# Attention on one core: half a slot of logits placed ahead of the value products, and the end of a query tile taken off ScalarE

## The chip, the cores and the metric

The kernel runs on one core of a Trainium2 chip. The metric is the device time of one execution in microseconds (us), as the median of several runs. The core has five engines with a queue each: TensorE (PE, matrix products; its weight loads are shown apart as PEld), VectorE (DVE), ScalarE (ACT), GpSimd (POOL) and SyncE (SP, which issues the DMAs here). Each engine works through its own queue in order, and semaphores tie the queues together.

## What is computed

The input x has the shape (2, 256, 64, 64): 2 images of 256 channels and 4096 tokens. Layer 0 is a Mamba block with an MLP; the change does not touch it. Layer 1 is attention with 8 heads of 32 channels, and this is what the change is about:

```python
x = x + _L0_conv_ref(_gn(x), ...)
x = x + _L1_conv_ref(_gn(x), qkv_w, qkv_b, 8)
...
qkv = jnp.einsum('bchw,oc->bohw', x, qkv_w) + qkv_b[None, :, None, None]
attn_logits = jnp.einsum('bhci,bhcj->bhij', q, k) * scale
attn_weights = jax.nn.softmax(attn_logits, axis=-1)
out = jnp.einsum('bhij,bhcj->bhci', attn_weights, v)
```

The kernel takes exponentials of the scaled logits without subtracting a maximum, sums them, and divides the value products by the sums at the end of a tile. A check of the range at the very end (`out_of_range`) starts a slower version if a sum was too large.

## The kernel before

`mamba_stage` runs first and fills about 2100 us. Then `attention_block` runs once for each image. Inside it, `prepare` normalises x and projects it to q, k and v; q and k go through DRAM, v stays in SBUF. What follows is one long loop of slots, and the change is in this loop.

**Tiles and slots.** A block has KG = 2 groups of four heads and NT = 8 query tiles of T = 512 queries, so 16 query tiles. Each tile goes through NC = 32 chunks of 128 keys. One slot s is one chunk of one tile: i is the tile, c the chunk. There are S = 512 slots in a block and 1024 in all.

**The work of one slot.**
- `logits(s)` (L952): on TensorE four products of keys and queries (L963), one for each head of the group, each 128 keys by 512 queries. Two heads share one PSUM tile `s`; the pool `ps_s` has two such tiles (L830), one for heads 0-1 and one for heads 2-3 in turn.
- `exponentials(s)` (L972): on ScalarE two activations (L977), each over two heads (128 x 1024), from a tile `s` into a tile `e`. The pool `ep` has six tiles `e` (L845), so those of three slots.
- `values(s)` (L980): on TensorE the products of v with `e` (L986), one for each head, added up over the 32 chunks in one PSUM tile `po` (one buffer, `ps_o`). The profile shows each of them as two matmuls, so eight for a slot.
- `add_up(s)` (L995): the sums of exponentials. DVE adds the `e` of heads 0-1 to `acc` (L1007). POOL adds the `e` of heads 2-3 to `acc_p` (L1018); in the 13 slots of `SHARED`, POOL takes one head of it (L1016) and DVE the other (L1015).

**The end of a tile.** `finish(i)` (L1020) is a generator; `side.run()` (L1074) advances it by one `yield` a slot, or two slots later where it yields 2. Its steps: copy `acc` (DVE, L1026), add the shared parts (DVE, L1027, which reads POOL's `acc_p`), copy `po` (ScalarE, L1029), and start the load of `res`, the old x (SP, L1031). Then sum over the partitions by products with ones (TensorE, L1036), copy the sums (DVE, L1039), and add the bias to `res` (ScalarE, L1040). Then reciprocals in four parts (DVE, L1047), `po` times the reciprocal (POOL, L1050), `res` plus `po` (POOL, L1052), and the store (SP, L1053).

**What sets the order.** Within `tc.manual_schedule()` the instructions of each engine stand in the order of the Python code, and the framework adds the semaphores. The loop (L1058 to L1078) issues for a slot s: on ScalarE both exponentials of s; on TensorE the values of s - 1, then a step of `finish` if one is due, then both halves of the logits of s + 1; then `add_up(s)`. When i is the last tile of the first group (i = 7), the keys of the next group are loaded as well, one piece every four slots (L1066). The SP queue carries these loads, the loads of queries (at c = 0, for the next tile) and those of `res`.

Of the kernel before, what the change touches and what calls it, by code (L numbers as in the profile page):

```python
# [13 lines left out]
AF = mybir.ActivationFunctionType  # L14
ALU = mybir.AluOpType
# [4 lines left out]
P = 128  # L20
# [793 lines left out]
def attention_block(ctx, tc, b, stats, consts, w, out, scratch, range_t):  # L814
# [5 lines left out]
    nc = tc.nc  # L820
    ident, gmat, _, eps_t = consts
    C, L = out.shape
    KC = C // P
    NT = L // T
    NC = L // P
    SCALE = 1.0 / math.sqrt(D)
# [10 lines left out]
    b_qkv = wp.tile([P, 3 * KC], F32, name="b_qkv")  # L837
# [4 lines left out]
    p1 = ctx.enter_context(tc.tile_pool(name=f"l1p1{b}", bufs=1))  # L842
    p2 = ctx.enter_context(tc.tile_pool(name=f"l1p2{b}", bufs=2))
    kp = ctx.enter_context(tc.tile_pool(name=f"l1k{b}", bufs=NT + 1))
    ep = ctx.enter_context(tc.tile_pool(name=f"l1e{b}", bufs=6))  # L845
    keys = {}
    queries = {}

    def load_keys(g, t):
        k = keys[g, t] = kp.tile([P, 4, T], F32R, name="k")  # L850
        load_stack(nc, k, scratch.qk[b * KG + g, 1, t], 1)

    def load_queries(i):
        if i < KG * NT:
            g, t = divmod(i, NT)
            q = queries[i] = p2.tile([P, 4, T], F32R, name="q")
            load_stack(nc, q, scratch.qk[b * KG + g, 0, t], 0)

    def s_tile():
        return ps_s.tile([P, 2, T], F32, name="s", tag="s")  # L860
# [79 lines left out]

    class Slot:
        pass

    S = KG * NT * NC
    SHARED = range(6, NC, 2)
    todo = {}
    tiles = {}
    side = Slots()  # L950

    def logits(s):  # L952
        if s >= S:
            return
        i, c = divmod(s, NC)
        kt, kj = divmod(c * P, T)
        d = todo[s] = Slot()
        d.s = []
        for half in range(2):
            ps = s_tile()  # L960
            for j in range(2):
                h = 2 * half + j
                nc.tensor.matmul(  # L963
                    ps[:, j, :],
                    lhsT=keys[i // NT, kt][:, h, kj : kj + P],
                    rhs=queries[i][:, h, :],
                    start=True,
                    stop=True,
                )
            d.s.append(ps)  # L970

    def exponentials(s):  # L972
        d = todo[s]
        d.e = []
        for half in range(2):
            e = ep.tile([P, 2, T], F32, name="e")
            nc.scalar.activation(e, d.s[half], AF.Exp, scale=SCALE)  # L977
            d.e.append(e)

    def values(s):  # L980
        i, c = divmod(s, NC)
        g = i // NT
        if c == 0:
            tiles[i].po = ps_o.tile([P, T], F32, name="po")
        for h in range(4):
            nc.tensor.matmul(  # L986
                tiles[i].po[h * D : (h + 1) * D, :],
                lhsT=v[:, c, g * P + h * D : g * P + (h + 1) * D],
                rhs=todo[s].e[h // 2][:, h % 2, :],
                start=(c == 0),  # L990
                stop=(c == NC - 1),
            )
        del todo[s]

    def add_up(s):  # L995

        i, c = divmod(s, NC)
        tile_ = tiles[i]
        ea, eb = todo[s].e
        if c == 0:  # L1000
            tile_.acc = ps_a.tile([P, 2, T], F32, name="acc")
            tile_.acc_p = p2.tile([P, 2, T], F32, name="acc_p")
            nc.vector.tensor_copy(tile_.acc, ea)
            tile_.eb0 = eb
            return
        acc, acc_p = tile_.acc, tile_.acc_p
        nc.vector.tensor_add(acc, acc, ea)  # L1007
        if c == 1:
            nc.gpsimd.tensor_add(acc_p, tile_.eb0, eb)  # L1009
        elif c in SHARED:  # L1010
            if c == SHARED[0]:
                tile_.acc_2 = ps_2.tile([P, T], F32, name="acc_2", tag="a2")
                nc.vector.tensor_copy(tile_.acc_2, eb[:, 0, :])
            else:
                nc.vector.tensor_add(tile_.acc_2, tile_.acc_2, eb[:, 0, :])  # L1015
            nc.gpsimd.tensor_add(acc_p[:, 1, :], acc_p[:, 1, :], eb[:, 1, :])  # L1016
        else:
            nc.gpsimd.tensor_add(acc_p, acc_p, eb)  # L1018

    def finish(i):  # L1020

        g, t = divmod(i, NT)
        d = tiles[i]
        cols = bass.ts(t, T)
        acc = p1.tile([P, 3, T], F32, name="acc_sb")
        nc.vector.tensor_copy(acc[:, 0:2, :], d.acc)  # L1026
        nc.vector.tensor_add(acc[:, 2, :], d.acc_2, d.acc_p[:, 0, :])  # L1027
        po = p1.tile([P, T], F32, name="po_sb")
        nc.scalar.copy(po, d.po)  # L1029
        res = p2.tile([P, T], F32, name="res")  # L1030
        nc.sync.dma_start(res, x[g * P : (g + 1) * P, cols])  # L1031
        yield
        ps = ps_2.tile([P, T], F32, name="sums_ps", tag="a2")
        for h in range(4):
            part = acc[:, h, :] if h < 3 else d.acc_p[:, 1, :]
            nc.tensor.matmul(ps[h * D : (h + 1) * D, :], lhsT=ones, rhs=part, start=True, stop=True)  # L1036
        yield
        sums = p1.tile([P, T], F32, name="sums")
        nc.vector.tensor_copy(sums, ps)  # L1039
        nc.scalar.activation(res, res, AF.Identity, bias=b_qkv[:, 2 * KC + g : 2 * KC + g + 1])  # L1040
        yield
        at = b * KG * NT + i
        nc.vector.tensor_reduce(range_t[:, 0, at : at + 1], sums, AX.X, ALU.max)
        yield 2
        r = p1.tile([P, T], F32, name="r")
        for j in range(T // P):
            nc.vector.reciprocal(r[:, bass.ts(j, P)], sums[:, bass.ts(j, P)])  # L1047
            yield 2
        nc.vector.tensor_reduce(range_t[:, 1, at : at + 1], r, AX.X, ALU.max)
        nc.gpsimd.tensor_mul(po, po, r)  # L1050
        yield 2
        nc.gpsimd.tensor_add(res, res, po)  # L1052
        nc.sync.dma_start(out[g * P : (g + 1) * P, cols], res)  # L1053

    with tc.manual_schedule():
        logits(0)
        s = 0
        while s <= S or side.waiting:  # L1058
            i, c = divmod(s, NC)
            if s < S:  # L1060
                if c == 0:
                    tiles[i] = Slot()
                    load_queries(i + 1)
                if i % NT == NT - 1 and i < KG * NT - 1 and c % (T // P) == 0:

                    load_keys(i // NT + 1, c * P // T)  # L1066
                exponentials(s)
            if 1 <= i <= KG:
                nc.sync.dma_start(scratch.v[b * KG + i - 1, :, c, :], v[:, c, (i - 1) * P : i * P])
            if 0 < s <= S:  # L1070
                values(s - 1)
                if c == 0:
                    side.start(side.now, finish(i - 1))
            side.run()  # L1074
            logits(s + 1)
            if s < S:
                add_up(s)
            s += 1  # L1078
# [99 lines left out]
@with_exitstack  # L1178
def conv_preact_kernel(ctx: ExitStack, tc: tile.TileContext, x: bass.AP, w: dict, out: bass.AP):
    nc = tc.nc  # L1180
    B, C, L = x.shape
    KC = C // P
    NT = L // T

    const = ctx.enter_context(tc.tile_pool(name="const", bufs=1))
    ident = const.tile([P, P], F32, name="ident")
    make_identity(nc, ident)
    gmat = const.tile([P, P], F32, name="gmat")
    nc.sync.dma_start(gmat, w["group_mean"])
    lnmat = const.tile([P, P], F32, name="lnmat")  # L1190
    nc.vector.memset(lnmat, 1.0 / C)
    eps_t = const.tile([P, 1], F32, name="eps_t")
    nc.vector.memset(eps_t, EPS)
    consts = (ident, gmat, lnmat, eps_t)

    scratch = Scratch(ctx.enter_context(tc.tile_pool(name="scratch", bufs=1, space=DRAM)), B * KG, L)
    range_t = const.tile([P, 2, B * KG * NT], F32, name="range_t")
    stats1 = [const.tile([P, KC, NT, nc.vector.BN_STATS_DIM], F32, name=f"stats1{b}") for b in range(B)]
    mamba_stage(tc, [x[b] for b in range(B)], stats1, consts, w, [scratch.image(b) for b in range(B)])
    for b in range(B):  # L1200
        attention_block(tc, b, stats1[b], consts, w, out[b], scratch, range_t)
    flag = out_of_range(tc, range_t)
    with tc.If(flag > 0):
        attention_any_range(tc, consts, w, out, scratch)
# [51 lines left out]
```

## Time and profile before

| | |
|---|---|
| median of 3 runs | 4630.29 us (4627.62 to 4630.42) |
| profiled execution | 4629.66 us, its span 4627.8 us |
| attention slots, from the first to the last exponential | 2192.5 to 3346.9 us and 3456.7 to 4610.0 us |
| ScalarE exponential L977, 128 x 1024 | 2048 times, 1024 ns each |
| TensorE logits L963 / values L986 | 4096 times 436 ns / 8192 times 605 ns |
| POOL additions L1018 / L1016 | 544 times 2392 ns / 416 times 1286 ns |
| DVE additions L1007 / L1015 | 992 times 1230 ns / 384 times 690 ns |
| copy of po L1029 and bias L1040 on ScalarE | 32 times 593 ns, 32 times 724 ns |
| last addition L1052 on POOL | 32 times 1292 ns |

How to read the profile: busy times are those of instructions on an engine; matmuls are pipelined and their ends are modelled, so their starts say more than their lengths. A row of the timeline gives the start, the length, the engine, the line, the operation, what it writes and reads, and how many of it were merged; in brackets stands how long the engine was idle before and who ended that. `issue` is a wait that the profile puts down to nobody. In the view of the waits a row gives the total, the number of times and the longest wait, in us.

### The profile page before, as it was taken

Reading aid. Unit: us, or ns where it says so; the run is one execution under the profiler, and the core shown is the slowest. Engines: PE = TensorE matmul, PEld = TensorE weight load, DVE = VectorE, ACT = ScalarE, POOL = GpSimd, SP = SyncE. Lnnn points to the kernel's source line nnn. Section 1 sums busy time; section 2 is a strip of 40 time slices with the busy share of each in tenths; the row PEclk is TensorE's granted clock in tenths of the full one; section 3 lists DMA queues with packets and bytes.
Section 4 is the critical chain, followed back from the end, with each engine's and each line's share of the span. In section 5 each row is a group of like instructions: output and inputs, shape, how many; then the busy total and the mean of one; then the engine's idle time right before and its main releaser. Section 6 shows DMA issues by size and latency. Waiting matters only on the chain.

```text
span 4627.8 us, 55923 instructions
## 1 busy us (share of the span) xinstructions
PE 4313.7 (93%) x18530; PEld 1572.5 (34%) x18530; DVE 3651.3 (79%) x3916; ACT 3690.4 (80%) x4860; POOL 3909.6 (84%) x2283
## 2 busy tenths in 40 slices
PE   5799999999999999888999999999989999999998
PEld 2233333333333333324333333333343333333332
DVE  3999999999999999964777767777747777777776
ACT  3778888888888888742888888888838888888887
POOL 1999999999999999960888888888818888888887
PEclk9899999999999999989999999999999999999999
DMA  5333333333333333308210140101091110401010
GB/s 169 107 106 107 112 121 119 123 123 124 123 124 118 116 119 124 113 34 264 68 44 17 26 98 19 26 17 26 10 265 33 44 25 20 98 17 26 21 26 8
DMA packets 162331, 379.67 MB, mean 82 GB/s; under 512 B 23409, under 2 KB 41585, under 8 KB 153841
## 3 DMA queue, kind: packets, MB, share of 16 engines
q1 hardware_dynamic: 162032, 376.03, 26.8%
q8 instruction: 147, 2.41, 0.2%
q14 instruction: 152, 1.24, 0.1%
HBM read 282.64 MB, written 93.32 MB: 81 GB/s over the span
## 4 chain that ended last, share of the span: by engine, by line
PE 59%; POOL 14%; DVE 10%; issue 7%; ACT 6%; DMA 4%; SPq 1%; POOLq 0%; DVEq 0%; ACTq 0%
PE s L963 25%; PE po L986 20%; POOL h L727 7%; DVE h L721 6%; PE mm L403 5%; POOL dbu L716 4%; PE y L753 2%; ACT e L977 2%; DMA xn<-x_dram 2%; PE mm L599 1%; PE mm L635 1%; PE s L887 1%; DVE bn L716 1%; ACT da L710 1%; ACT L234 1%
## 5 line engine op out<-in xcount | busy, mean ns | idle before, releaser
L977 ACT ACTIVATE e<-s 128x1024 f32<-128x1024 f32 x2048 | 1988.8, 1024 | 284.6 <-PE s L963 282.0
L1007 DVE TENSOR_TENSOR acc<-acc,e 128x1024 f32<-128x1024 f32 x992 | 1220.4, 1230 | 567.9 <-ACT e L977 564.7
L1018 POOL TENSOR_TENSOR acc_p<-acc_p,e 128x1024 f32<-128x1024 f32 x544 | 1301.3, 2392 | 226.6 <-ACT e L977 213.2
L963 PE MATMUL s<-q,k 128*128 128x512 f32 x4096 | 1322.6, 436 | 13.3 <-ACT e L977 10.4
L727 POOL TENSOR_TENSOR h<-h,c 128x1024 f32<-128x1024 f32 x512 | 1205.4, 2367 | 17.7 <-ACT state L724 12.3
L986 PE MATMUL po<-e,v 128*32 128x512 f32 x8192 | 1093.8, 605 | 0.0
L963 PEld LDWEIGHTS s<-q,k 128*128 128x128 f32 x4096 | 617.0, 188 | 1131.6 <-ACT e L977 1123.0
L710 ACT ACTIVATE da<-dt_rep,neg_a 128x512 f32<-128x512 f32 x1024 | 692.8, 702 | 126.3 <-DVE h L721 106.8
L721 DVE TENSOR_TENSOR_SCAN h<-da,state,dbu 128x512 f32<-128x512 f32 x512 | 650.6, 1275 | 77.5 <-POOL dbu L716 73.7
L721 DVE TENSOR_TENSOR_SCAN h<-da,state,bn 128x512 f32<-128x512 f32 x512 | 648.4, 1267 | 13.7
L1016 POOL TENSOR_TENSOR acc_p<-acc_p,e 128x512 f32<-128x512 f32 x416 | 534.9, 1286 | 32.8 <-POOL acc_p L1018 0.2
L716 POOL TENSOR_TENSOR dbu<-dtu_rep,b 128x512 f32<-128x512 f32 x384 | 487.3, 1280 | 8.8 <-DMA dtu_rep<-dtu_dram 7.4
L234 ACT ACT_TABLE_LOAD x331 | 424.7, 1283 | 6.6 <-PEq L1246 0.7
L403 PE MATMUL bn<-proj,pick 112*128 112x512 f32 x512 | 305.3, 612 | 124.7 <-DVE h L721 124.4
L753 PE MATMUL y<-h,sum 128*32 128x512 f32 x2048 | 381.2, 639 | 38.3 <-POOL h L727 37.9
L716 DVE TENSOR_TENSOR bn<-dtu_rep,bn 128x512 f32<-128x512 f32 x512 | 349.8, 683 | 37.7 <-DMA dtu_rep<-dtu_dram 20.1
L1009 POOL TENSOR_TENSOR acc_p<-e 128x1024 f32<-128x1024 f32 x32 | 76.5, 2392 | 272.0 <-ACT e L977 272.0
L986 PEld LDWEIGHTS po<-e,v 128*32 128x32 f32 x8192 | 161.7, 108 | 375.3 <-issue 361.9
L403 PE MATMUL mm<-yn,w_in 128*128 128x512 f32 x512 | 260.2, 633 | 11.0 <-ACT yn L492 5.2
L1015 DVE TENSOR_TENSOR acc<-acc,e 128x512 f32<-128x512 f32 x384 | 264.9, 690 | 0.0
L403 PE MATMUL mm<-xm,taps 128*128 128x512 f32 x512 | 236.7, 606 | 16.2 <-POOL xm L539 14.1
L403 PE MATMUL mm<-yn,w 128*128 128x512 f32 x512 | 240.4, 599 | 10.6 <-ACT z L587 9.3
(126 smaller groups left out, 3477.0 us busy)
## 6 DMA issues: line engine op xcount, KB each, us to landing
dt_rep<-dt_dram SPq DMA_DIRECT2D x128, 512.0 KB, 5.2
dtu_rep<-dtu_dram SPq DMA_DIRECT2D x128, 512.0 KB, 5.7
qk_dram<-halves SPq DMA_DIRECT2D x64, 512.0 KB, 5.7
q<-qk_dram SPq DMA_DIRECT2D x128, 256.0 KB, 4.9
k<-qk_dram SPq DMA_DIRECT2D x64, 512.0 KB, 7.5
b<-bc_dram SPq DMA_DIRECT2D x64, 256.0 KB, 3.1
c<-bc_dram SPq DMA_DIRECT2D x64, 256.0 KB, 4.1
dt_dram<-dt SPq DMA_DIRECT2D x64, 256.0 KB, 2.0
```

Of the source, the lines that this page charges most:

```text
L403: nc.tensor.matmul(out, lhsT=lhsT, rhs=rhs, start=(i == 0), stop=(i == len(pairs) - 1))
L710: nc.scalar.activation(da[j].tile, dt.tile[:, j, :], AF.Exp, scale=scale)
L716: engine.tensor_mul(out.tile, dtu.tile[:, j, :], rows.tile)
L721: nc.vector.tensor_tensor_scan(h.tile[:, j, :], da[j].tile, dbu.tile, initial, ALU.mult, ALU.add)
L727: nc.gpsimd.tensor_tensor(h.tile, h.tile, rows_c.tile.unsqueeze(1).to_broadcast([P, 2, T]), ALU.mult)
L753: nc.tensor.matmul(y.tile[j * PQ : (j + 1) * PQ, :], lhsT=sum4, rhs=pair[j // 2].h.tile[:, j % 2, :], start=False, stop=(qd == NQ - 1),)
L963: nc.tensor.matmul(ps[:, j, :], lhsT=keys[i // NT, kt][:, h, kj : kj + P], rhs=queries[i][:, h, :], start=True, stop=True,)
L977: nc.scalar.activation(e, d.s[half], AF.Exp, scale=SCALE)
L986: nc.tensor.matmul(tiles[i].po[h * D : (h + 1) * D, :], lhsT=v[:, c, g * P + h * D : g * P + (h + 1) * D], rhs=todo[s].e[h // 2][:, h % 2, :],
L1007: nc.vector.tensor_add(acc, acc, ea)
L1016: nc.gpsimd.tensor_add(acc_p[:, 1, :], acc_p[:, 1, :], eb[:, 1, :])
L1018: nc.gpsimd.tensor_add(acc_p, acc_p, eb)
```

## The change

The functions `logits` and `exponentials` take the half (heads 0-1 or heads 2-3) as an argument. Before the loop, the logits of slot 0, the exponential of its first half and the first half of the logits of slot 1 are issued. In the loop ScalarE gets the second half of s and then the first half of s + 1. TensorE gets the values of s - 1, then the second half of the logits of s + 1, then the first half of those of s + 2. The pool `ep` gets a seventh tile.

In `finish`, the copy of `po` goes to DVE, behind L1027. The bias addition on ScalarE is gone; the last step is one DVE instruction, po + bias + res, in place of POOL's addition.

```diff
-    ep = ctx.enter_context(tc.tile_pool(name=f"l1e{b}", bufs=6))
+    ep = ctx.enter_context(tc.tile_pool(name=f"l1e{b}", bufs=7))
...
-    def logits(s):
+    def logits(s, half):
         if s >= S:
             return
...
-    def exponentials(s):
-        d = todo[s]
-        d.e = []
-        for half in range(2):
+        if half == 0:
+            todo[s] = Slot()
+            todo[s].s, todo[s].e = [], []
+        ps = s_tile()
+        for j in range(2):
+            h = 2 * half + j
+            nc.tensor.matmul(
+                ps[:, j, :], lhsT=keys[i // NT, kt][:, h, kj : kj + P], rhs=queries[i][:, h, :], start=True, stop=True
+            )
+        todo[s].s.append(ps)
+
+    def exponentials(s, half):
+        if s < S:
             e = ep.tile([P, 2, T], F32, name="e")
-            nc.scalar.activation(e, d.s[half], AF.Exp, scale=SCALE)
-            d.e.append(e)
+            nc.scalar.activation(e, todo[s].s[half], AF.Exp, scale=SCALE)
+            todo[s].e.append(e)
...
         po = p1.tile([P, T], F32, name="po_sb")
-        nc.scalar.copy(po, d.po)
+        nc.vector.tensor_copy(po, d.po)
...
-        nc.scalar.activation(res, res, AF.Identity, bias=b_qkv[:, 2 * KC + g : 2 * KC + g + 1])
...
-        nc.gpsimd.tensor_add(res, res, po)
+        bias = b_qkv[:, 2 * KC + g : 2 * KC + g + 1]
+        nc.vector.scalar_tensor_tensor(res, po, bias, res, ALU.add, ALU.add)
         nc.sync.dma_start(out[g * P : (g + 1) * P, cols], res)
 
     with tc.manual_schedule():
-        logits(0)
+        logits(0, 0)
+        logits(0, 1)
+        exponentials(0, 0)
+        logits(1, 0)
...
-                exponentials(s)
+                exponentials(s, 1)
+                exponentials(s + 1, 0)
...
             side.run()
-            logits(s + 1)
+            logits(s + 1, 1)
+            logits(s + 2, 0)
```

More of the change, by code (lines that the diff above doesn't have):

```diff
@@ L956, in logits @@
         kt, kj = divmod(c * P, T)
-        d = todo[s] = Slot()
-        d.s = []
-        for half in range(2):
[L960 to L970, printed above, removed]
-    def exponentials(s):
-        d = todo[s]
-        d.e = []
-        for half in range(2):
+        if half == 0:
[10 more added lines that the diff above has]
+        if s < S:
             e = ep.tile([P, 2, T], F32, name="e")
-            nc.scalar.activation(e, d.s[half], AF.Exp, scale=SCALE)
-            d.e.append(e)
+            nc.scalar.activation(e, todo[s].s[half], AF.Exp, scale=SCALE)
+            todo[s].e.append(e)
     def values(s):
```

## The prediction, on record before the result

> **What bounds the kernel now.** I first read the page: busy shares, then the chain that ended last.
>
> ```profile
> PE 4313.7 (93%) x18530; PEld 1572.5 (34%) x18530; DVE 3651.3 (79%) x3916; ACT 3690.4 (80%) x4860; POOL 3909.6 (84%) x2283
> ...
> PE s L963 25%; PE po L986 20%; POOL h L727 7%; DVE h L721 6%; PE mm L403 5%; POOL dbu L716 4%; PE y L753 2%; ACT e L977 2%; DMA xn<-x_dram 2%; PE mm L599 1%; PE mm L635 1%; PE s L887 1%; DVE bn L716 1%; ACT da L710 1%; ACT L234 1%
> ```
>
> No engine is full over the whole span. The two attention lines on TensorE (logits L963, value products L986) carry 45% of the chain; the rest belongs mostly to the Mamba stage, which the change leaves alone. Next, the view of the waits from 2200 us on, where attention runs:
>
> ```profile
> PEld s L963 <- ACT e L977: 1119.9, 1977, 5.5
> ...
> ACT e L977 <- PE s L963: 280.5, 927, 1.9
> ```
>
> TensorE waits for ScalarE and ScalarE for TensorE: neither engine alone, but a loop through both. Its size comes from the timeline in the middle of a tile (start, length, engine, line; DVE and POOL rows left out):
>
> ```profile
> 2941.20 1.20 PE L963 MATMUL s<-q,k 128*128 128x512 f32 x4
> 2941.65 0.31 PEld L963 LDWEIGHTS s<-q,k 128*128 128x128 f32 x2 [0.16 <-ACT e L977]
> 2941.97 1.94 ACT L977 ACTIVATE e<-s 128x1024 f32<-128x1024 f32 x2 [0.37 <-PE s L963]
> ...
> 2942.32 1.06 PE L986 MATMUL po<-e,v 128*32 128x512 f32 x8
> 2943.32 0.30 PEld L963 LDWEIGHTS s<-q,k 128*128 128x128 f32 x2 [0.84 <-ACT e L977]
> ...
> 2943.96 0.30 PEld L963 LDWEIGHTS s<-q,k 128*128 128x128 f32 x2 [0.34 <-ACT e L977]
> 2944.09 1.94 ACT L977 ACTIVATE e<-s 128x1024 f32<-128x1024 f32 x2 [0.18 <-PE s L963]
> ...
> 2944.62 1.07 PE L986 MATMUL po<-e,v 128*32 128x512 f32 x8
> 2945.61 0.30 PEld L963 LDWEIGHTS s<-q,k 128*128 128x128 f32 x2 [0.84 <-ACT e L977]
> ```
>
> Call the first pair of logits after a value block F, the second G. The starts give: F to G 0.45 (2941.65 - 2941.20), G to values 0.67, values to next F 1.00. That is 2.12 us a slot for TensorE alone. The next slot takes 2.29, because its G starts at 2943.96, 0.05 after the second exponential ended (2941.97 + 1.94 = 2943.91). The exponential fed by F starts 0.77 after F (2944.09 - 2943.32), the other 0.92 later. So the loop is: G to values 0.67, values to F 1.00, F to its exponential 0.77, both exponentials 1.94, handover 0.05 = 4.43 us for two slots, 2.21 a slot. ScalarE alone would need 2 x 0.92 = 1.84.
>
> **What the Trainium skill says.** "TensorE: Matmul & The Clock Gate", Part 1: the array falls to half clock after about 3.4 us without work; the table of windows agrees (0.50 below, after a stall of 4.70). The same page, table at its head: ScalarE's queue is strictly first in, first out. The trace agrees: an exponential behind the bias addition L1040 starts only 0.62 after it. "Perfetto Trace Analysis", Identifying Dependency Chains: an instruction that waits for several engines can get separate event-semaphore instructions ahead of it. The trace has them: 17 ns records ahead of exponentials. "ScalarE: Activation LUTs", What ACT_TABLE_LOAD costs: back-to-back activations overlap by 0.09 us, here 1.02 long and 0.92 apart.
>
> **The change, part by part.** *Running ahead by half a slot.* ScalarE's order of exponentials stays the same (heads 0-1, 2-3, 0-1, ...). On TensorE a value block now stands between heads 0-1 and 2-3 of a slot instead of ahead of both. Then F is heads 2-3 and G is heads 0-1 of the next slot. F still needs the buffer freed two exponentials earlier, G likewise, and there are still two buffers. The loop just worked out contains no name of a head: with the names swapped it has the same five terms, 4.43. The value block gains half a slot of slack in its inputs, but it never waited for them: ahead of L986 the view lists 361.2 us of "issue", 2.4 on exponentials. So I put zero on this part. The earlier heads 0-1 also read q and k half a slot sooner; both are loaded a tile ahead. Its price from both sides: if G stopped waiting, 1024 x (2.215 - 2.12) = 97 us gained; if the first exponential needed one more queue wait, two such records in a row start 0.09 us apart in the trace: 512 x 0.09 = 46 lost.
>
> *Seven buffers e instead of six.* Buffer k is reused seven exponentials later, so a half follows the other half. The early half then inherits POOL's release and the late one DVE's. Before, heads 0-1 (F's exponential) waited for TensorE and DVE, heads 2-3 also for POOL. After, heads 2-3 (F's again) wait for TensorE and DVE. The same wait falls on the same place: zero. Lifetime: a buffer is now held half a slot longer and there is one half more.
>
> *ScalarE's bias addition L1040 (32 x 0.725 us) goes.* On 28 tile ends its cost is a delay of one exponential:
>
> ```profile
> 2923.66 0.73 ACT L1040 ACTIVATE res<-res,b_qkv 128x512 f32<-128x512 f32 x1
> ...
> 2924.28 3.92 ACT L977 ACTIVATE e<-s 128x1024 f32<-128x1024 f32 x4
> ```
>
> F stood at 2923.19, so the exponential was due at 2923.96: 0.32 late. The sums' eight matmuls (L1036) add 0.85 to one slot (values 2919.22 to F 2921.07 is 1.85 instead of 1.00). From the exponentials' starts, an ordinary tile is 71.77 us and 16 loops are 70.8: a tile end costs 0.97 = 0.85 + 0.32 - 0.20, the last being what the slack of a slot without a wait (2.29 - 2.12 = 0.17) takes up. Afterwards 0.85 stays and 0.32 goes.
>
> On the two tile ends during which the next group's keys are loaded (i = 7 of each block) it costs more:
>
> ```profile
> 2695.86 10.64 DMA res<-x_dram
> ```
> ```profile
> 2630.00:2702.00 72.00, 71.96 (x394) 24.63 (x394) 54.02 (x55) 63.07 (x67) 62.25 (x34) 1.00 0.13 30
> 2702.00:2706.50 4.50, 1.60 (x10) 0.33 (x10) 0.76 (x2) 0.00 (x0) 2.33 (x1) 0.98 1.04 226
> 2706.50:2712.50 6.00, 4.29 (x13) 1.57 (x14) 3.21 (x3) 4.55 (x5) 3.21 (x2) 0.50 0.40 89
> ```
>
> The load of res (median 2.8 us) lands after 10.64 behind the keys; L1040 waits, ScalarE is idle for 4.5 us (fourth busy column 0.00), and TensorE then runs 6 us at clock 0.50. These tiles took 78.39 and 77.94 us against 71.77: 6.62 + 6.17 = 12.8 us. In the new code res is first read some 15 slots (33 us) into the tile. All 12.8 go; if the slow clock stayed, 2 x 4.7 = 9.4.
>
> *The copy of po moves from ScalarE (0.59) to DVE.* On ScalarE it cost nothing:
>
> ```profile
> 2918.39 0.59 ACT L1029 COPY po_sb<-po 128x512 f32<-128x512 f32 x1
> 2918.55 0.30 PEld L963 LDWEIGHTS s<-q,k 128*128 128x128 f32 x2 [0.16 <-ACT e L977]
> 2918.86 1.96 ACT L977 ACTIVATE e<-s 128x1024 f32<-128x1024 f32 x2
> 2918.95 0.69 DVE L1027 TENSOR_TENSOR acc_sb<-acc,acc_p 128x512 f32<-128x512 f32 x1 [0.95 <-POOL acc_p L1018]
> 2919.22 0.16 PEld L986 LDWEIGHTS po<-e,v 128*32 128x32 f32 x8 [0.36 <-ACT po_sb L1029]
> ```
>
> The exponential at 2918.86 is where F (2918.09) + 0.77 puts it, the values at 2919.22 are G + 0.67. On DVE the copy stands behind L1027, which waits for POOL, and the new tile's first value block waits for the copy. Count from the start of slot 31's last exponential (here 2914.44 + 0.92 = 2915.36): L1027 starts at 3.59, what follows it 0.61 later (2919.55 in an earlier timeline row, acc<-e L1003), so 4.20; a copy of this form takes 0.68 (L1039): 4.88; TensorE at 4.93. In the new order G waits for the exponential after that one: 0.92 + 1.02 + 0.05 = 1.99, plus 0.66 gives slot 31's values at 2.65, and the new tile's first values 2.12 to 2.30 later: 4.77 to 4.95. The copy's input is complete at 2.65 + 1.3 = 3.95 and holds DVE up not at all. TensorE, with the sums and the next F queued behind and ScalarE waiting for F, waits 0 to 0.16; after a slot without a wait, which the alternation gives here, 0. I take 0.02. A new tile end is then 0.85 + 0.02 = 0.87, a gain of 0.10; bounds: slack used in full, 0.65 (gain 0.32), and the wait in full, 1.01 (loss 0.04). 28 x 0.10 = 2.8, from 9.0 to -1.1; the two key tiles add 0.2.
>
> *POOL's addition (1.29) becomes one DVE instruction* (0.69 to 0.75, from L1015 and L898). It waits for POOL's multiplication, issued two slots (4.4 us) earlier, with accumulations queued behind it; the store of res on SP's queue waits for DVE in place of POOL, no longer than before: zero. DVE goes from 3651 to about 3697 busy us and stays idle a quarter of attention; lateness of the accumulations is covered by three slots of e buffers. Without that cover each 0.7 would fall on ScalarE: 32 x 1.4 = 45. At the very end of the program it shortens the tail by 1.29 - 0.75 less a handover: 0.4.
>
> **Sum:** 12.8 + 0.2 + 2.8 + 0.4 = 16.2 us. The profiled execution took 4629.66 (span 4627.8), 0.6 under the median of 4630.29; less 16.2 it gives 4613.5 and for the median **4614**. Own range of this case: 4630.3 - 22.6 = 4608 to 4630.3 - 8.3 = 4622 (slow clock kept, wait in full).
>
> **Rivals.** *Late copy (0.10).* DVE reaches the copy later than I think, by one more operation of 0.6: 30 x 0.6 = 18 eats the gain: about 4632. For it: the margin at 4.93 against 4.95 is nil. Against it: DVE stood idle 0.95 ahead of L1027, and only POOL sets it. *Slower (0.11).* The first exponential after the values gets its waits in two instructions because the rotation of seven mixes releases of PE, DVE and POOL: 0.09 on each of 512 loops, 46 - 16 = 30 lost: 4660; it decides from 16 / 512 = 0.03 us a loop. For it: the exponentials already carry such records; against: they mirror exactly. *Faster (0.09).* The loop opens and TensorE alone sets 2.12: 97 + 13 gained, 4520. For it: the 0.17 wait ahead of G in every second slot; against: G's buffer still comes from the exponential just before. That the running ahead does nothing is my forecast itself **(0.70)**.
>
> About 0.2% (9.3 us) is what a measurement of this kernel can tell from no change. Faster: 0.68 of the forecast's 0.70 and the 0.09: 0.77; same: 0.02 + 0.10 = 0.12; slower: 0.11. The range takes the forecast and the late copy, 4607 to 4633, and leaves 0.20 out.
>
> **What would show it.** Right: two-slot loop still 4.43 with G 0.05 behind an exponential; tiles i = 7 at about 71.7 and no clock of 0.50 there; other tiles 71.6 to 71.8; ACT busy down by 32 x (0.59 + 0.725) = 42 us. Wrong: slots of 2.12 (faster rival) or F to its exponential above 0.80 (slower); values of slot 0 starting over 0.1 us after G + 0.67 with DVE as releaser (late copy).

## The result, and the profile after

The changed kernel takes 4615.31 us (median of 4 runs, 4612.46 to 4615.83) against 4630.35 of the kernel before in the same runs: ratio 0.9967, 95% interval 0.9950 to 0.9984. That is 15 us, or 0.33%; 16 were forecast. The profiled execution took 4614.82 us, its span 4613.0.

Busy shares and the chain of the page, after:

```profile
PE 4311.6 (93%) x18530; PEld 1571.9 (34%) x18530; DVE 3725.3 (81%) x3980; ACT 3659.2 (79%) x4796; POOL 3883.1 (84%) x2251
...
PE s L964 27%; PE po L981 22%; DVE h L721 6%; POOL h L727 6%; PE mm L403 6%; POOL dbu L716 3%; PE y L753 2%; PE mm L599 2%; PE mm L635 2%; PE s L887 1%; DVE bn L716 1%; DMA xn<-x_dram 1%; PE bn L403 1%; ACT da L710 1%; DMA dtu_rep<-dtu_dram 1%
```

The lines have moved by a few (logits L964, values L981, exponentials L972). ScalarE lost 31 us of busy time, DVE gained 74, and the chain has the same owners. The mutual wait is as large as before:

```profile
PEld s L964 <- ACT e L972: 1109.9, 2005, 1.7
...
ACT e L972 <- PE s L964: 302.7, 1018, 2.0
```

Only the longest waits have gone: 1.7 us in place of 5.5. The timeline in the middle of a tile:

```profile
2938.17 0.31 PEld L964 LDWEIGHTS s<-q,k 128*128 128x128 f32 x2 [0.16 <-ACT e L972]
2938.49 1.94 ACT L972 ACTIVATE e<-s 128x1024 f32<-128x1024 f32 x2 [0.37 <-PE s L964]
2938.83 0.16 PEld L981 LDWEIGHTS po<-e,v 128*32 128x32 f32 x8 [0.35 <-issue]
...
2939.83 0.30 PEld L964 LDWEIGHTS s<-q,k 128*128 128x128 f32 x2 [0.84 <-ACT e L972]
...
2940.48 0.30 PEld L964 LDWEIGHTS s<-q,k 128*128 128x128 f32 x2 [0.35 <-ACT e L972]
2940.60 1.94 ACT L972 ACTIVATE e<-s 128x1024 f32<-128x1024 f32 x2 [0.17 <-PE s L964]
```

It is the same rhythm. The second pair of logits, G, is loaded at 2940.48, 0.05 after the exponentials that began at 2938.49 ended (2940.43). F to its exponential is 0.77 again (2940.60 - 2939.83). Over the tiles the median loop of two slots is 4.423 us, before it was 4.424.

The windows that held the stall of a key tile, taken at the same times:

```profile
2702.00:2706.50 4.50, 4.50 (x28) 1.58 (x32) 3.41 (x4) 3.96 (x5) 4.34 (x3) 1.00 0.79 169
2706.50:2712.50 6.00, 6.00 (x35) 1.90 (x28) 5.32 (x7) 5.32 (x6) 5.76 (x4) 1.00 0.55 127
```

TensorE (first busy column) is busy throughout and its clock is 1.00, while the key loads keep the DMA engines 79% busy. The changed kernel reaches this tile some 4 us earlier; in windows moved by 4.1 us the DMA engines are as full as before (1.05 against 1.04), with TensorE still busy throughout at clock 1.00. The load of res is as late as it was: in the two key tiles it lands 9.6 and 10.7 us after its issue. The starts of the exponentials give the tiles: 71.60 us for both key tiles (78.39 and 77.94 before) and 71.59 to 71.66 for the others but the first of each block (71.77 before).

### The profile page after: what moved, and what is told of

It reads as the page before. It is cut to its first block, busy times and chain, and to the rows that moved or that the text cites. A ratio compares the mean times of both kernels' runs of the same rounds, so it can differ in the third digit from the quotient of the medians.

```text
span 4613.0 us, 55891 instructions
## 1 busy us (share of the span) xinstructions
PE 4311.6 (93%) x18530; PEld 1571.9 (34%) x18530; DVE 3725.3 (81%) x3980; ACT 3659.2 (79%) x4796; POOL 3883.1 (84%) x2251
## 4 chain that ended last, share of the span: by engine, by line
PE 65%; POOL 11%; DVE 10%; issue 6%; ACT 3%; DMA 3%; SPq 0%; POOLq 0%; DVEq 0%; ACTq 0%
PE s L964 27%; PE po L981 22%; DVE h L721 6%; POOL h L727 6%; PE mm L403 6%; POOL dbu L716 3%; PE y L753 2%; PE mm L599 2%; PE mm L635 2%; PE s L887 1%; DVE bn L716 1%; DMA xn<-x_dram 1%; PE bn L403 1%; ACT da L710 1%; DMA dtu_rep<-dtu_dram 1%
## 5 line engine op out<-in xcount | busy, mean ns | idle before, releaser
L972 ACT ACTIVATE e<-s 128x1024 f32<-128x1024 f32 x2048 | 1987.1, 1022 | 305.2 <-PE s L964 305.0
L1002 DVE TENSOR_TENSOR acc<-acc,e 128x1024 f32<-128x1024 f32 x992 | 1219.4, 1229 | 407.5 <-ACT e L972 404.4
L964 PE MATMUL s<-q,k 128*128 128x512 f32 x4096 | 1317.4, 435 | 3.8 <-ACT e L972 2.1
L981 PE MATMUL po<-e,v 128*32 128x512 f32 x8192 | 1092.0, 605 | 0.0
L964 PEld LDWEIGHTS s<-q,k 128*128 128x128 f32 x4096 | 614.0, 188 | 1120.2 <-ACT e L972 1114.5
L1011 POOL TENSOR_TENSOR acc_p<-acc_p,e 128x512 f32<-128x512 f32 x416 | 548.0, 1317 | 33.0 <-POOL acc_p L1013 0.6
L981 PEld LDWEIGHTS po<-e,v 128*32 128x32 f32 x8192 | 161.6, 108 | 373.2 <-issue 361.9
```

The costliest lines, as they stand in the source:

```text
L964: nc.tensor.matmul(ps[:, j, :], lhsT=keys[i // NT, kt][:, h, kj : kj + P], rhs=queries[i][:, h, :], start=True, stop=True)
L972: nc.scalar.activation(e, todo[s].s[half], AF.Exp, scale=SCALE)
L981: nc.tensor.matmul(tiles[i].po[h * D : (h + 1) * D, :], lhsT=v[:, c, g * P + h * D : g * P + (h + 1) * D], rhs=todo[s].e[h // 2][:, h % 2, :],
```

## The experiments

Each run is compared with the kernel before on the same chip; the ratio is what counts, since the kernel before had medians from 4626.7 to 4628.3 us beside them.

**One part alone.** Three kernels divide the change.

`e1_ahead_only`: the running ahead and seven buffers, with the old end of a tile.

```diff
-        nc.vector.tensor_copy(po, d.po)
+        nc.scalar.copy(po, d.po)
...
+        nc.scalar.activation(res, res, AF.Identity, bias=b_qkv[:, 2 * KC + g : 2 * KC + g + 1])
...
-        nc.vector.scalar_tensor_tensor(res, po, bias, res, ALU.add, ALU.add)
+        nc.gpsimd.tensor_add(res, res, po)
```

> The running ahead and the seventh buffer alone; the end of a tile is that of the kernel before. My theory: the loop of two slots stays at 4.42 us, since it is the same loop with the heads' names swapped; the bias addition on ScalarE still waits for res in the two key tiles (about 78 us each) and still delays one exponential in every tile; tiles 71.7 to 71.9. The time stays at that of the kernel before, 4626 to 4634. Rival, the running ahead is where the gain comes from: 4613 to 4620.

Measured: 4627.38 against 4627.04 us, ratio 1.000 (0.9991 to 1.0008). Loop 4.422, ordinary tiles 71.75, key tiles 77.96 and 77.70. The running ahead by itself gives nothing that can be measured.

`e2_finish_only`: the new end of a tile in the old order, with six buffers.

> The new end of a tile alone, in the old order and with six buffers. My theory: the first value block of a tile is due 3.86 us after the start of slot 31's last exponential in the old order, and DVE's copy of po is done at 4.93; TensorE waits about 1.07 at each tile end. Ordinary tiles about 72.6 (71.6 + 1.07), key tiles the same in place of 78; 28 x 0.9 - 2 x 5.6 + some 4 at the ends of the blocks: slower, 4640 to 4655. Rival, the running ahead does nothing at all and the end of a tile is the whole gain: 4613 to 4619.

Measured: 4643.61, ratio 1.0031 (1.0021 to 1.0042), tiles 72.57, key tiles 72.54 and 72.57. The tile end on its own:

```profile
2917.51 0.30 PEld L963 LDWEIGHTS s<-q,k 128*128 128x128 f32 x2 [0.34 <-ACT e L977]
...
2918.34 0.68 DVE L1029 COPY po_sb<-po 128x512 f32<-128x512 f32 x1
...
2919.08 0.16 PEld L986 LDWEIGHTS po<-e,v 128*32 128x32 f32 x8 [1.27 <-DVE po_sb L1029]
```

The values were due 0.66 after G, at 2918.17, and start at 2919.08: TensorE waits 0.91 for DVE's copy. So the end of a tile without ScalarE, put into the old order, loses more than it wins: with the copy of po on DVE the order matters.

`e3_bias_only`: the kernel before, with only L1040 taken away and POOL's last addition replaced by the DVE instruction with the bias. The copy of po stays on ScalarE.

> Only the bias addition leaves ScalarE (one DVE instruction adds po, bias and res at the end); the copy of po stays on ScalarE, the order and the six buffers are those of before. My theory: this alone is the gain: key tiles 71.6 in place of 78, ordinary tiles 71.6 in place of 71.77, no wait of TensorE for po: 4612 to 4619, the same as the whole change. Rival, the copy of po or the running ahead is needed as well: 4622 to 4630.

Measured: 4615.42, ratio 0.9971 (0.9959 to 0.9983); tiles 71.67, key tiles 71.65 and 71.69. This one edit has all of the gain that can be measured, in the old order. Its tiles are 0.06 longer than those of the whole change (71.61), under 2 us in all, which the times can't tell apart.

**Where the gain comes from.** In the kernel before, the addition of the bias in a key tile shows its wait:

```profile
2706.52 0.72 ACT L1040 ACTIVATE res<-res,b_qkv 128x512 f32<-128x512 f32 x1 [4.70 <-DMA res<-x_dram]
```

`e6_bias_late` moves L1040 down in the old kernel and changes nothing else:

```diff
-        nc.scalar.activation(res, res, AF.Identity, bias=b_qkv[:, 2 * KC + g : 2 * KC + g + 1])
...
         nc.gpsimd.tensor_mul(po, po, r)
+        nc.scalar.activation(res, res, AF.Identity, bias=b_qkv[:, 2 * KC + g : 2 * KC + g + 1])
```

> The kernel before with one line moved: ScalarE's bias addition stands some ten slots later, beside POOL's multiplication, when res has long landed. My theory: the key tiles lose their stall (71.8 in place of 78), while every tile keeps a delayed exponential: 0.1 to 0.2 more a tile than with the bias off ScalarE; 13 us under the kernel before, ratio 0.997. Rival, the key loads themselves stall the tile: key tiles stay near 78 and the time that of before.

Measured: 4616.29, ratio 0.9975 (0.9965 to 0.9985); key tiles 71.76 and 71.77, the others 71.76. ScalarE still does all its work, the keys are still loaded, and res still lands 10.9 and 9.8 us after its issue in the key tiles. So the late load did harm only through the place of the addition that waits for it: neither ScalarE's work nor the key loads by themselves stall a tile. With `e3` the rest is seen too: 71.76 against 71.67, so the addition itself costs 0.09 a tile.

**The wait on the first exponential.** `e4_six_e` is the whole change with `bufs=6`.

> The whole change, but six buffers e in place of seven, so that each half takes over buffers of the same half; the first exponential after the values then has POOL's release to wait for beside TensorE's, in two instructions. My slower rival priced this at 0.09 us a loop. Expected: loop of two slots 4.48 to 4.52, 512 x 0.06 to 0.09: 4645 to 4662. If a second queue wait costs nothing there: 4.42 and 4613 to 4618.

Measured: 4643.98, ratio 1.0034 (1.0022 to 1.0046); loop 4.483. The timeline of this kernel:

```profile
2936.33 0.30 PEld L964 LDWEIGHTS s<-q,k 128*128 128x128 f32 x2 [0.84 <-ACT e L972]
...
2937.15 1.94 ACT L972 ACTIVATE e<-s 128x1024 f32<-128x1024 f32 x2 [0.16 <-issue]
```

F to its exponential is 0.82 in place of 0.77, and the idle time is now put down to "issue". The semaphores in the two traces show what differs. In both kernels the first exponential after the values has separate instructions ahead of it for some of its waits. With seven buffers the exponential itself waits for TensorE, and the separate instruction, for DVE, is long past. With six the exponential itself nearly always waits for POOL, and the separate instruction takes TensorE's release, which comes last: outside the shared slots it starts 0.06 us ahead of the exponential (604 times; in the kernel with seven buffers never). 0.06 x 512 loops = 31 us, near the 4644 - 4615 = 29 measured; the expectation began at 4645. The seventh buffer is what makes the running ahead free.

**What closes the loop.** `e7_three_s` gives a third PSUM tile to the logits; to make room, `acc` moves to SBUF.

```diff
-    ps_s = ctx.enter_context(tc.tile_pool(name=f"l1pss{b}", bufs=2, space=PSUM))
-    ps_a = ctx.enter_context(tc.tile_pool(name=f"l1psa{b}", bufs=1, space=PSUM))
+    ps_s = ctx.enter_context(tc.tile_pool(name=f"l1pss{b}", bufs=3, space=PSUM))
...
-            tile_.acc = ps_a.tile([P, 2, T], F32, name="acc")
+            tile_.acc = p1.tile([P, 2, T], F32, name="acc")
...
-        res = p2.tile([P, T], F32, name="res")
+        res = p1.tile([P, T], F32, name="res")
```

> The whole change, with acc in SBUF and the two PSUM banks that this frees given to a third tile s (res has one buffer for room). My theory of the loop: G then needs a buffer freed an exponential earlier, the loop through both engines opens, and TensorE alone sets the slot: two slots 4.24, tiles 68.7 to 69.1 (with some wait for DVE's copy of po), 32 x 2.6 to 2.9 under the whole change: 4522 to 4540. Rival, something else holds the slots (ScalarE, DVE or POOL, or the additions in SBUF are slower): two slots stay above 4.35 and the time above 4580.

`e8_three_s_old_order` is the same on top of `e3` (with `res` unchanged).

> Third tile s and acc in SBUF, with the old order, six buffers e, the copy of po on ScalarE and only the bias off ScalarE. My theory: the running ahead gives nothing here either; two slots 4.24, tiles 68.6 to 69.0, 4520 to 4537. Rival, the running ahead pays once the loop is open: over 10 us slower than the same with the running ahead.

Measured: 5374.29 (ratio 1.1613, 1.1597 to 1.1629) and 5353.23 (1.1569, 1.1553 to 1.1585). Both theories missed by over 800 us; what came true is the rival of `e7_three_s`, slower additions in SBUF, which said no more than a time above 4580. The groups of `e8_three_s_old_order` from 2200 us on:

```profile
L1006 DVE TENSOR_TENSOR acc<-acc,e 128x1024 f32<-128x1024 f32 x979 | 2323.6, 2373 | 139.8 <-ACT e L976 90.9 <-DVE acc L1006 0.9 <-DVE acc L1002 0.5
L976 ACT ACTIVATE e<-s 128x1024 f32<-128x1024 f32 x2021 | 1978.2, 1025 | 1000.4 <-DVE acc L1006 519.5 <-PE s L962 311.4 <-POOL acc_p L1017 150.8
L1017 POOL TENSOR_TENSOR acc_p<-acc_p,e 128x1024 f32<-128x1024 f32 x538 | 1674.8, 3113 | 238.8 <-ACT e L976 202.7
```

DVE's addition went from 1230 to 2373 ns and POOL's from 2392 to 3113, now that both of DVE's inputs lie in SBUF; then ScalarE waits for both to free `e`. It is not SBUF alone: the 31 additions of DVE in this trace during which no POOL instruction ran took 1225 ns, as short as those in PSUM, while those that POOL overlapped for 70 to 99% of their length had a median of 2435. The Trainium skill has this ("SBUF — State Buffer", SBUF: two separate sides): DVE instructions with two SBUF inputs and GpSimd instructions that read SBUF share a port pair that one of them holds at a time. The measured lengths agree in direction. Yet for five or six slots early in each tile, mostly from the fourth on, a slot took 2.12 us: there the loop had opened. To see it without that cost, the next two leave out DVE's additions L1002 altogether, so the sums of heads 0-1 lack 31 of 32 slots.

`e9_no_add_two_s`: two tiles s.

> The whole change with DVE's additions of the exponentials of heads 0-1 left out (only slot 0's copy stays), so the sums of these heads lack 31 of 32 slots; a control for the next. My theory: DVE's additions are not in the loop: two slots 4.42, tiles 71.3 to 71.7, 4605 to 4617. Rival, DVE's additions in PSUM hold the slots: two slots below 4.35.

Measured: 4644.98, ratio 1.0037 (1.0023 to 1.0051), loop 4.482, F to its exponential 0.83. The expectation missed by 0.06 a loop. The trace shows why: without DVE's release the first exponential itself waits for ScalarE's own earlier write, and a separate instruction 0.06 ahead of it takes TensorE's release (986 times), as in `e4_six_e`. It was not the additions that held the slots: leaving out 1220 us of DVE's work made nothing faster.

`e10_no_add_three_s`: three tiles s.

> The same omission with acc in SBUF and a third PSUM tile s, so without the slow additions in SBUF. My theory: the loop opens and TensorE alone sets the slot: two slots 4.24 and tiles 68.7 to 69.1; 4518 to 4540. Rival, two PSUM tiles s are not what closes the loop: two slots stay at 4.42, 4605 to 4617.

Measured: 4530.46, ratio 0.9791 (0.9775 to 0.9806); loop 4.240 and tiles 69.10. Against `e9` that is 115 us, of which about 31 are the separate wait of `e9`; 84 are left. The open loop alone is worth 512 x (4.423 - 4.240) = 94, and tile ends that cost 0.4 more here (69.10 - 16 x 4.240 = 1.26, against 71.61 - 16 x 4.423 = 0.84 in the changed kernel) take some 12 of it back. So what held the slots is the number of PSUM tiles that the exponentials give back, and beyond it TensorE alone.

**A version faster than both.** Nothing is left out in `e11_one_head`. The four PSUM banks are kept, as four tiles of one head, with one exponential for each:

```diff
+        for h in (2 * half, 2 * half + 1):
+            ps = ps_h.tile([P, T], F32, name="s")
+            nc.tensor.matmul(
+                ps, lhsT=keys[i // NT, kt][:, h, kj : kj + P], rhs=queries[i][:, h, :], start=True, stop=True
+            )
+            todo[s].s.append(ps)
...
+            for j in range(2):
+                nc.scalar.activation(e[:, j, :], todo[s].s[2 * half + j], AF.Exp, scale=SCALE)
```

> The whole change with the bias alone on DVE, and four PSUM tiles s of one head in place of two of two heads, in the same four banks, with one exponential (128 x 512) a head. Nothing is left out. My theory: the third pair of logits then waits for one exponential of 0.6 in place of one of 1.02, the loop falls below TensorE's 4.24 for two slots; ScalarE needs 4 x about 0.51 = 2.05 a slot against TensorE's 2.12. Two slots 4.24 to 4.30, 4520 to 4560. Rival, four shorter exponentials and their waits make ScalarE the bound: two slots 4.40 or more, 4610 or slower.

Measured: 4524.68, ratio 0.9776 (0.9762 to 0.9790). Its timeline:

```profile
2935.74 5.82 ACT L973 ACTIVATE e<-s 128x512 f32<-128x512 f32 x11
...
2937.33 0.76 PEld L964 LDWEIGHTS s<-q,k 128*128 128x128 f32 x4 [0.84 <-ACT e L973]
...
2938.45 0.16 PEld L982 LDWEIGHTS po<-e,v 128*32 128x32 f32 x8 [0.37 <-issue]
...
2939.45 0.76 PEld L964 LDWEIGHTS s<-q,k 128*128 128x128 f32 x4 [0.84 <-ACT e L973]
```

All four logits of a slot run in one stretch (x4, no wait between the pairs) and a slot takes 2.12 us (2939.45 - 2937.33). ScalarE does twice the instructions (604 ns each, in groups without a gap) and still keeps pace.

`e12_one_head_old_order` is the same in the old order of values and logits, with six buffers and the copy of po on ScalarE.

> Four one-head PSUM tiles s with one exponential a head, in the old order of value products and logits, six buffers e, the copy of po on ScalarE, the bias alone on DVE: no part of the running ahead. My theory: in the middle of a tile TensorE sets 2.12 a slot here too, since the values' inputs are ready in time; ScalarE's copy of po (0.59 in every tile, with some 0.07 us of slack a slot) costs 0 to 0.5 a tile, 4522 to 4542. Rival, the half slot of slack is needed once the loop is open: slots above 2.2 and 4560 or more.

Measured: 4522.61, ratio 0.9775 (0.9762 to 0.9789); slots 2.12, tiles 68.72 (`e11`: 68.88). Running ahead by half a slot is of no use with the loop open either.

**The ends of the blocks.** `e5_bias_dve` splits the last step: DVE adds the bias to `res`, POOL adds `po`.

> The whole change, but the last step is split: DVE adds the bias to res (waits for nobody late), POOL adds po as in the kernel before. DVE then no longer waits for POOL's multiplication at the end of a block. My theory: tiles as with the whole change (71.6); the way from the last exponential to the end falls from 20.2 us to 18.8 or less, and between the blocks the wait for POOL ahead of the next block's normalisation goes (some 2 us): 2 to 5 us under the whole change, 4610 to 4613 against a kernel before of 4630. If the ends of the blocks are unaffected: equal to the whole change.

Measured: 4609.85, ratio 0.9966 (0.9952 to 0.9979), which can't be told from the whole change's 0.9967. Tiles 71.61. The way from the last exponential to the end did not fall: 20.8 us. This expectation missed: DVE's addition of the bias took 0.99 there and the comparison L1092 1.14, in place of 0.18 in the changed kernel, beside POOL's multiplication and addition. That the two engines held each other up there is an argument, not a test. Between the blocks, from the last exponential of the first to the first of the second, it was 108.1 us, against 113.8 in the changed kernel. But `e4_six_e`, with the changed kernel's tile end, has 109.3, so this shows nothing about the wait for POOL.

## Why the prediction was right, point by point

**The loop is a renaming: zero.** Right. 4.423 against 4.424, and `e1` gives 1.000. The rival in which the loop opens fell; `e10` shows what would have opened it, and its price (4.24) is the 2.12 a slot that the prediction read from TensorE's starts.

**Seven buffers put the same wait in the same place.** Right, and tested from the other side: with six, the slower rival's mechanism appears. Its price was 0.09 a loop; it is 0.06.

**Key tiles: 12.8.** Measured: 6.79 + 6.34 = 13.1. The prediction counted these tiles down to 71.77 and the 0.2 apart, so 13.0 in its terms. The slow clock went with the stall. Two of its readings are off without touching the term. The median of 2.8 us for the load of res is that of its loads and stores taken together; the 32 loads alone have 5.7. An ordinary tile thus escaped the wait narrowly: in the one shown with L1040 at 2923.66, the load was issued at 2917.15 and landed 0.7 us before the addition began. And the two waits are 8.9 us together, not 2 x 4.7.

**Ordinary tile ends: 0.10 each.** 0.16 measured (71.77 to 71.61), so 28 x 0.16 = 4.5 in place of 2.8. The bias alone gives the 0.10 (`e3`: 71.67). The other 0.06 comes with the copy of po and the new order, of which the order alone gives 0.02 (`e1`: 71.75): on DVE the copy cost nothing, and on ScalarE it seems to have cost a little, where the prediction had nothing. The tile end of the changed kernel:

```profile
2979.58 0.69 DVE L1022 TENSOR_TENSOR acc_sb<-acc,acc_p 128x512 f32<-128x512 f32 x1 [1.25 <-POOL acc_p L1013]
...
2980.19 0.68 DVE L1024 COPY po_sb<-po 128x512 f32<-128x512 f32 x1
2980.27 0.30 PEld L964 LDWEIGHTS s<-q,k 128*128 128x128 f32 x2 [0.34 <-ACT e L972]
...
2980.93 0.16 PEld L981 LDWEIGHTS po<-e,v 128*32 128x32 f32 x8 [0.36 <-DVE po_sb L1024]
```

The copy ends at 2980.87, the values start at 2980.93, which is G + 0.66: no wait, by a margin of nothing, as the prediction had it (4.93 against 4.95). That margin is all that the running ahead buys: in `e2` the same copy is late by 0.91. Two changes that look independent are a pair: the later value block pays for the copy on DVE. But the copy never had to leave ScalarE (`e3`).

**The tail: 0.4 gained.** Wrong in sign, and the one term that failed. From the start of the last exponential to the end it was 18.8 us before and is 20.2 after: 1.4 lost. The prediction compared the lengths of two last instructions and took the store behind them for the end. The store does start 0.5 earlier (12.4 after that exponential in place of 13.0). But the end goes with the check of the range, which also stands in DVE's queue: from the end of the check's last DVE instruction it is 6.3 us before and 6.4 after, and 6.0 to 6.7 in all kernels here, while from the start of the store it varies from 5.8 to 8.0. Before, DVE checked the range while POOL multiplied and added. After, the check waits behind DVE's new instruction, which waits for POOL's multiplication: from the start of the range reduction (L1049, after L1043) to the next step of the check (L1090) it took 0.72 before and takes 2.14, and that is the 1.4.

Between the blocks the same wait holds up the next block's normalisation (`gn_e`), as the chain of the changed kernel shows:

```profile
3345.26 1.26 POOL po_sb L1044
3346.55 0.75 DVE res L1047
3347.30 0.14 DVE gn_e L46
```

From the range reduction's start to the product with `gn_e` it took 1.37 before (3356.20 to 3357.57) and 2.29 after (3345.20 to 3347.49). The gap between the blocks' exponentials grew from 110.8 to 113.8; it varies from 107.6 to 114.2 among the kernels here, with the loads of `xn` on its chain, so at most 0.9 of the 3.0 is laid to this wait. The prediction had no term for this gap.

**Busy times.** The 42 us less on ScalarE that the prediction named as a sign came out as 31. The two lines' 42 us are gone (23.2 + 19.0), but the page counts time in which two instructions overlap once, and these two overlapped their neighbours. DVE gained 74 in place of 46: its instructions are 44 us longer in all, and they overlap 30 us less.

**The sum.** In the profiled executions the slots of the two blocks took 9.2 and 7.2 us less: 13.1 + 4.5, less 1.2 in the first and last tiles of the blocks. The ends took back 1.4 and 3.0, and the first exponential, before which the change touches next to nothing, came 2.7 earlier. That makes 14.7; the spans differ by 14.8, and 16.2 was forecast. The forecast is right by its main term, the key tiles; that the total comes so close is in part luck, since a gain in the tile ends and an earlier start that nobody forecast made up for the ends of the blocks.

## What to carry to other kernels

Before reordering a loop across two engines, write it as a list of handovers without the operands' names; if the list is the same afterwards, so is the period, as long as the waits fall on the same instructions (`e4_six_e` has the same list and lost 0.06 a loop). What opens it is one more buffer or a smaller piece (here four PSUM tiles of one head in place of two of two: 2.2%). An instruction that needs a late DMA should not stand in the queue of an engine on the loop, whatever its own length: two waits of 8.9 us together cost 13. Moving work to an idle engine has to be checked against what stands behind it in that queue, at the ends of the stages too.

## What the runs showed of the hardware that was not expected

- DVE's addition of two 128x1024 float32 operands takes 1230 ns with one of them in PSUM and on average 2373 ns with both in SBUF beside POOL, whose own goes from 2392 to 3113 ns; with both in SBUF and POOL idle it takes 1225 ns. The whole change has a trace of this: its new DVE instruction reads two SBUF operands, and the 30 of POOL's 416 additions L1011 that it overlaps took 0.4 us longer each, which no instruction waited for.
- Which of an activation's waits a separate instruction takes has a price: where it is the release that comes last, the activation starts 0.06 us later, even if the release that the activation itself waits for is long past (4.483 against 4.423 a loop, in two kernels). Where the separate instruction takes an earlier release, no such delay is seen.
- Two exponentials of 128x512 in place of one of 128x1024 cost ScalarE 2115 us of busy time (`e11`) in place of 1989, and the kernel still became 2.2% faster.
